# State and gate products of a gated state-space convolution block, issued as four 32x32 tiles each instead of one 32x128 tile

## The chip, the cores and the metric

The kernel runs on one core of one Trainium2 chip. The metric is the device time of one execution, in microseconds (us). The core has a matrix engine (TensorE, PE in the profile, with its weight loads shown apart as PEld), VectorE (DVE), ScalarE (ACT), GpSimd (POOL) and SyncE (SP), which issues the DMAs.

## The reference

The input x is 4 images of 128 channels of 96 x 96. It is normalised in groups of four channels, and then goes through the same one-dimensional block in four reading orders (rows, rows reversed, columns, columns reversed). The four results are joined by a 1x1 convolution and added to x. The block is, shortened:

```python
t = grouped1x1(x, in_proj_w, in_proj_b, 4)             # 128 -> 512 channels, 4 groups
u, gate = t[:, :256], t[:, 256:]
u = depthwise_conv5(silu(u), dw_w)
s = ssm_in_w @ u                                       # 32 channels
a = 0.999 + 0.0009 * sigmoid(ssm_delta_w @ u + ssm_delta_b)
bb, cc = tanh(ssm_b_w @ u + ssm_b_b), tanh(ssm_c_w @ u + ssm_c_b)
h = linear_scan(a, bb * s)                             # h[t] = a[t] h[t-1] + bb[t] s[t]
u = u + ssm_out_w @ (cc * h + ssm_d * s)               # 32 -> 256 channels: the state product
u = grouped1x1(u * sigmoid(gate), mix_w, mix_b, 4)     # gate: the gate product
return out_proj_w @ u
```

Mixing, output projection and joining are linear and stand behind each other, so the kernel multiplies their weights once (`w_fin`) and has one product per direction for them.

## The kernel before, in words

**Tiles.** A direction and its reverse are worked on together as sides s = 0 and 1. The sequence is cut into 384-element pieces, with four interleaved phases; one piece of both sides is a pair, and there are 192 pairs. All data are f32. Psum is one tile of eight banks, which the code rents out to named tenants (`TENANTS`, `BANKS`) and takes back when the last user has been written down.

**Products on PE.** A product writes 128 output channels of one bank. Most are issued through the helper `mm` (line 245), which writes 32 of them, so that four instructions make one product:

- the input projection F (`in_proj`), 32 input rows by 32 output columns a tile, 385 elements,
- the convolution C and its rest L (`conv`, `conv_less`), 128x32 and 64x32,
- the projections P to the small state (`proj`), 128x32,
- the last product W (`result`, weights `w_fin`), 128x32.

The state product S (`state`, line 866) and the gate product G (`gate`, line 872) are the exceptions: one instruction each, 32 input rows by all 128 output columns. A pair has four state products (S00, S01, S10, S11), on the four row groups of the array, each to its own bank. Half of the pairs also have four gate products (G00 to G11), again on the four row groups; for the other half the gates were stored and come back by DMA. ACT copies u to psum ahead of the state products (`under`, line 862), so that these add to it.

**Behind them.** ACT's `tanh_gate` (line 878) reads a gate product. DVE's `gating` (line 919) reads a pair of state products and multiplies by the gate; its result is what W reads one slot later. ACT's `take_result` (line 932) copies W's result, and POOL adds it to the output (line 972).

**Order.** Nothing is scheduled by a tool. The program is a list of slots, one for each pair, and in each slot a written order of operations (`PLAN`, four kinds of slot) is issued with a lag for each operation (`LAGS`); the start and the end have lists of their own (`START`, `END`). Each engine takes its instructions in the order in which they were issued, and semaphores hold what isn't ready. In the kind "gate" the part of the order that concerns PE reads `S11 S10 G00 S00 G01 G11 S01 G10`, then `W11 W10`: eight products of 32x128 in one stretch, on row groups 3, 1, 2, 0 and again 3, 1, 2, 0. In the kinds "front" and "none" the four state products of a pair stand together, without gate products.

## Time and profile before

| | |
|---|---|
| time, median of 3 runs | 1776.74 us (1774.55 to 1778.56) |
| span of the profiled execution, first to last instruction | 1770.6 us |
| mean granted TensorE clock | 0.994 |
| PE busy | 1747.7 us (99%) |
| DVE, ACT, POOL busy | 1516.8, 1486.1, 1394.0 us |
| matmul records on PE | 22584 |
| of these state products (L866) | 1536 records, 257.4 us busy |
| of these gate products (L872) | 768 records, 187.9 us busy |

The profiled execution's own time isn't told apart from the other runs; what lies around its span is the difference to them, 6.1 us at the median. In a row such as `128*32 128x384` the first pair is the tile's size on the array (rows by columns), the second the output. Busy time of a group is the union of its instructions, so where several run side by side it is far less than their count times the mean. A matmul of f32 is two records, its two passes, and each has a weight load of its own.

### The profile page before, as it was taken

The numbers are of one execution on the slowest core, as the hardware profiler recorded it, in microseconds if no ns is written. First come the engines' busy times: TensorE is split into PE (matmuls) and PEld (weight loads), VectorE is DVE, ScalarE is ACT, GpSimd is POOL, SyncE is SP. The second block draws the span as 40 slices with busy tenths as digits, with TensorE's granted clock in tenths as the row PEclk, the third lists the DMA queues.
The fourth block names the chain that finished last, engine by engine and source line by source line (L and its number), as shares of the span: only waits on it lengthen the run. The fifth ranks groups of instructions, "written<-read, shape, count | busy, mean of one in ns | idle before, by whom it ended". The sixth has DMA issues, their size and how long they took to land.

```text
span 1770.6 us, 54587 instructions
## 1 busy us (share of the span) xinstructions
PE 1747.7 (99%) x22584; PEld 638.7 (36%) x22584; DVE 1516.8 (86%) x1541; ACT 1486.1 (84%) x2571; POOL 1394.0 (79%) x1500
## 2 busy tenths in 40 slices
PE   6999999999999999999999999999999999999999
PEld 3333333333333333333333333333333333333333
DVE  4899988888788988988888988898888878888898
ACT  5788888888888888888888888888888888888875
POOL 4488888878778888788877888878777788887776
PEclk7999999999999999999999999999999999999999
DMA  7776676665987678564798657755589755656654
GB/s 229 180 238 232 180 227 187 201 204 175 295 261 235 209 209 241 182 204 165 218 293 264 231 188 227 223 179 198 165 257 278 250 193 181 209 159 198 215 190 165
DMA packets 183767, 377.69 MB, mean 213 GB/s; under 512 B 16736, under 2 KB 147040, under 8 KB 183520
## 3 DMA queue, kind: packets, MB, share of 16 engines
q1 hardware_dynamic: 183376, 374.16, 67.4%
q8 instruction: 178, 2.92, 0.7%
q14 instruction: 69, 0.57, 0.1%
q10 hardware_dynamic: 144, 0.04, 0.0%
HBM read 222.96 MB, written 151.18 MB: 211 GB/s over the span
## 4 chain that ended last, share of the span: by engine, by line
PE 91%; DMA 3%; ACT 2%; issue 1%; SPq 1%; DVE 1%; POOL 0%; ACTq 0%; POOLq 0%; DVEq 0%
PE psum L245 78%; PE psum L866 10%; PE psum L872 4%; DMA acc<-in_xr 2%; DMA out<-acc 1%; ACT gate L878 1%; POOL acc L972 0%; SPq L713 0%; DMA x_in<-in_xs 0%; ACT psum L862 0%; DVE u L919 0%; ACT sil L647 0%; DMA edge<-edge 0%; ACT u L748 0%; ACT t L812 0%
## 5 line engine op out<-in xcount | busy, mean ns | idle before, releaser
L785 DVE SCALAR_TENSOR_TENSOR psum<-sil,small,psum 128x768 f32<-128x768 f32 x576 | 588.1, 1022 | 56.1 <-ACT psum L783 38.1
L245 PE MATMUL psum<-u,w_fin 128*32 128x384 f32 x6144 | 580.0, 490 | 0.9
L245 PE MATMUL psum<-u,main 128*32 128x384 f32 x6144 | 562.2, 488 | 1.8 <-ACT gate L878 0.7
L972 POOL TENSOR_TENSOR acc<-ys,acc 128x384 f32<-128x384 f32 x365 | 422.1, 1165 | 155.2 <-ACT ys L932 76.8
L919 DVE SCALAR_TENSOR_TENSOR u<-gate,psum 128x768 f32<-128x768 f32 x376 | 346.0, 951 | 97.1 <-PE psum L866 69.9
L245 PEld LDWEIGHTS psum<-u,main 128*32 128x32 f32 x6144 | 186.6, 109 | 325.9 <-issue 216.0
L245 PEld LDWEIGHTS psum<-u,w_fin 128*32 128x32 f32 x6144 | 175.3, 109 | 342.8 <-issue 241.9
L862 ACT COPY psum<-u 128x768 f32<-128x768 f32 x352 | 278.1, 800 | 23.6 <-DVE u L766 8.4
L849 POOL TENSOR_TENSOR t<-t,t 64x384 f32<-64x384 f32 x192 | 235.1, 1225 | 68.4 <-DVE t L843 32.2
L245 PE MATMUL psum<-sil,band 128*32 128x384 f32 x3072 | 287.6, 490 | 1.1 <-ACT ys L932 1.1
L866 PE MATMUL psum<-t,main 32*128 32x384 f32 x1536 | 257.4, 530 | 1.3 <-ACT psum L862 1.3
L853 POOL TENSOR_TENSOR t<-t,t 64x384 f32<-64x384 f32 x192 | 236.9, 1234 | 7.6
L878 ACT ACTIVATE gate<-psum,bnorm 128x384 f32<-128x384 f32 x384 | 211.7, 577 | 33.4 <-PE psum L872 15.6
L826 POOL TENSOR_TENSOR t<-t,tm 64x384 f32<-64x384 f32 x191 | 196.0, 1026 | 51.1 <-ACT t L809 39.0
L823 POOL TENSOR_SCALAR t<-tm 64x384 f32<-64x384 f32 x191 | 179.7, 941 | 51.3 <-ACT tm L801 36.2
L647 ACT ACTIVATE sil<-psum,bnorm 128x385 f32<-128x385 f32 x384 | 200.4, 581 | 22.4 <-PE psum L245 21.8
L785 DVE SCALAR_TENSOR_TENSOR u<-sil,small,psum 128x768 f32<-128x768 f32 x192 | 194.7, 1014 | 18.2
L783 ACT ACTIVATE psum<-sil,small 128x768 f32<-128x768 f32 x192 | 173.7, 905 | 36.2 <-DVE u L919 31.5
L872 PE MATMUL psum<-x_in,wn 32*128 32x384 f32 x768 | 187.9, 516 | 0.2
L801 ACT ACTIVATE tm<-psum,small 128x384 f32<-128x384 f32 x192 | 112.5, 586 | 59.5 <-PE psum L245 57.2
L245 PEld LDWEIGHTS psum<-sil,band 128*32 128x32 f32 x3072 | 97.2, 110 | 152.4 <-issue 102.1
L932 ACT COPY ys<-psum 128x384 f32<-128x384 f32 x278 | 133.1, 479 | 21.3 <-POOL acc L972 10.9
(84 smaller groups left out, 1442.3 us busy)
## 6 DMA issues: line engine op xcount, KB each, us to landing
sil<-sil SPq DMA_DIRECT2D x128, 770.0 KB, 7.1
kept<-gate SPq DMA_DIRECT2D x80, 768.0 KB, 4.4
gate<-kept SPq DMA_DIRECT2D x76, 768.0 KB, 5.7
edge<-edge SPq DMA_DIRECT2D x96, 384.0 KB, 5.9
x_in<-in_xs SPq DMA_DIRECT2D x192, 96.2 KB, 3.5
edge<-sil SPq DMA_DIRECT2D x96, 192.5 KB, 3.9
acc<-in_xr SPq DMA_DIRECT2D x47, 384.0 KB, 7.8
out<-acc SPq DMA_DIRECT2D x44, 384.0 KB, 3.8
```

The costliest lines, as they stand in the source:

```text
L245: nc.tensor.matmul(o[r, : rhs.shape[-1]], lhsT, rhs, start=start, stop=stop, skip_group_check=True)
L647: nc.scalar.activation(sils[step][:, j, s, g, :], bank(frm)[:, : N + 1], AF.Silu, bias=bn[:, 1:2] if j else bn[:, 4 + g : 5 + g],)
L785: nc.vector.scalar_tensor_tensor(u_of(n)[:, :, 1, :] if k == K - 1 else part, src, w_tap[:, k : k + 1], part, ALU.mult, ALU.add,)
L826: engine.tensor_mul(scan_of(n)[0:64, pair_of(n)["p"], :], tbs[n][0:64, :], tms[n][0:64, :])
L849: engine.tensor_mul(ta[0:64, p, :], tbs[n][64:P, :], ta[64:P, p, :])
L853: engine.tensor_add(z, scans[n // R][0:64, pair_of(n)["p"], :], z)
L862: nc.scalar.copy(two(to), us[n][:, s])
L866: nc.tensor.matmul(bank(to)[:, :N], w_so[r, bass.ts(j, P)], tbs[n][r, :], start=not seeded(n), stop=True, skip_group_check=True)
L872: nc.tensor.matmul(bank(to)[:, :N], stats[pair_of(n)["b"]][0][r, s, :], x_in[s][r, q, off : off + N], start=True, stop=True)
L878: nc.scalar.activation(gates[n % 2][:, s, j, :], bank(frm)[:, :N], AF.Tanh, bias=bn[:, 2 + j : 3 + j], scale=0.5,)
L919: nc.vector.scalar_tensor_tensor(v, g, 1.0, two(frm), ALU.add, ALU.mult)
L972: nc.gpsimd.tensor_add(to, y, part)
```

## The change

Each state product and each gate product is issued as four tiles of 32 rows by 32 columns through `mm`, one for each quarter of the output channels. The operands, the banks, the place in the order and the flags of accumulation stay the same.

```diff
     def state(n, s, j, to):
         r = slice(64 * j + 32 * s, 64 * j + 32 * s + 32)
-        nc.tensor.matmul(bank(to)[:, :N], w_so[r, bass.ts(j, P)], tbs[n][r, :],
-                         start=not seeded(n), stop=True, skip_group_check=True)
+        for c in range(4):
+            mm(bank(to), c, w_so[r, j * P + 32 * c : j * P + 32 * c + 32], tbs[n][r, :],
+               not seeded(n), True)
 
     def gate(n, s, j, to):
         q, off = gate_at(pair_of(n))
         r = slice(64 * (1 - s) + 32 * j, 64 * (1 - s) + 32 * j + 32)
-        nc.tensor.matmul(bank(to)[:, :N], stats[pair_of(n)["b"]][0][r, s, :],
-                         x_in[s][r, q, off : off + N], start=True, stop=True)
+        for c in range(4):
+            mm(bank(to), c, stats[pair_of(n)["b"]][0][r, s, 32 * c : 32 * c + 32],
+               x_in[s][r, q, off : off + N], True, True)
```

On PE in a slot of the kind "gate", before: the run of eight products (t is the state, x_in with wn a gate product), between two pieces of W's work.

```order
L245 MATMUL psum<-u_732,w_fin 32x384 x4
L866 MATMUL psum<-t_5_913,main 128x384 x2
L872 MATMUL psum<-x_in_70,wn_330 128x384
L866 MATMUL psum<-t_5_913,main 128x384
L872 MATMUL psum<-x_in_70,wn_330 128x384
L872 MATMUL psum<-x_in_71,wn_330 128x384
L866 MATMUL psum<-t_5_913,main 128x384
L872 MATMUL psum<-x_in_71,wn_330 128x384
L245 MATMUL psum<-u_732,w_fin 32x384 x8
```

The same place on PE after the change:

```order
L245 MATMUL psum<-u_732,w_fin 32x384 x4
L245 MATMUL psum<-t_5_934,main 32x384 x8
L245 MATMUL psum<-x_in_70,wn_330 32x384 x4
L245 MATMUL psum<-t_5_934,main 32x384 x4
L245 MATMUL psum<-x_in_70,wn_330 32x384 x4
L245 MATMUL psum<-x_in_71,wn_330 32x384 x4
L245 MATMUL psum<-t_5_934,main 32x384 x4
L245 MATMUL psum<-x_in_71,wn_330 32x384 x4
L245 MATMUL psum<-u_732,w_fin 32x384 x8
```

Nothing has moved: eight instructions have become 32 at the same place, and the semaphores that a product waits for are on its first tile. On the other engines the order is the same as before.

On PE in slots of the kind "front", before: four state products in one run, between the convolution and its rest, and the projection F with 16 tiles close by.

```order
L245 MATMUL psum<-u_2918,main 32x384 x8
L245 MATMUL psum<-x_in_70,wn_330 32x385 x4
L245 MATMUL psum<-x_in_71,wn_330 32x385 x8
L245 MATMUL psum<-x_in_70,wn_330 32x385 x4
L245 MATMUL psum<-u_2918,main 32x384 x8
L245 MATMUL psum<-u_2289,w_fin 32x384 x8
L245 MATMUL psum<-sil_2596,band 32x384 x8
L866 MATMUL psum<-t_22_2490,main 128x384 x4
L245 MATMUL psum<-sil_2596,less 32x384 x8
```

After the change the row of L866 there is 16 tiles of line 245, the same number as F's 4 + 8 + 4 above it. Over the whole program PE's matmul instructions go from 11292 to 14748.

## The prediction

> **What bounds the kernel now.** I read the page's busy times first, then the chain that ended last, then the costliest groups.

> ```profile
> PE 1747.7 (99%) x22584; PEld 638.7 (36%) x22584; DVE 1516.8 (86%) x1541; ACT 1486.1 (84%) x2571; POOL 1394.0 (79%) x1500
> ...
> PE 91%; DMA 3%; ACT 2%; issue 1%; SPq 1%; DVE 1%; POOL 0%; ACTq 0%; POOLq 0%; DVEq 0%
> PE psum L245 78%; PE psum L866 10%; PE psum L872 4%; DMA acc<-in_xr 2%; DMA out<-acc 1%; ACT gate L878 1%; POOL acc L972 0%; SPq L713 0%; DMA x_in<-in_xs 0%; ACT psum L862 0%; DVE u L919 0%; ACT sil L647 0%; DMA edge<-edge 0%; ACT u L748 0%; ACT t L812 0%
> ...
> L866 PE MATMUL psum<-t,main 32*128 32x384 f32 x1536 | 257.4, 530 | 1.3 <-ACT psum L862 1.3
> L872 PE MATMUL psum<-x_in,wn 32*128 32x384 f32 x768 | 187.9, 516 | 0.2
> ```

> PE is busy 99% of the span and 91% of the chain. The changed products, L866 (state) and L872 (gate), are 10% and 4% of that chain. So what they gain or lose on PE goes almost straight into the time. The program has 768 state and 384 gate products, and the trace has 1536 and 768 records: each f32 product runs as two passes, each with its own weight load. After the change the 2304 pairs of load and matmul become 9216.

> How PE moves through such a run is the whole question. A run here is a stretch of instructions with one tile shape. Two runs can be compared directly: four state products of 32x128 (8 records), and 16 tiles of 32x32 in the projection F (32 records), which already has the form that state and gate products will get.

> ```profile
> 706.24 0.93 PE L866 MATMUL psum<-t,main 32*128 32x384 f32 x8
> 707.10 0.88 PE L245 MATMUL psum<-sil,less 64*32 64x384 f32 x16
> ...
> 701.36 0.95 PE L245 MATMUL psum<-x_in,wn 32*32 32x385 f32 x32
> 702.23 0.53 PE L245 MATMUL psum<-u,main 128*32 128x384 f32 x4
> ```

> The first column is the start, the second the length. From start to the start of the next shape the state run takes 707.10 - 706.24 = 0.86 us, the F run 702.23 - 701.36 = 0.87. So four products on four row groups cost the same array time in either form.

> **The change, term by term.**

> *Weight loads.* They get shorter and more numerous:

> ```profile
> L866 PEld LDWEIGHTS psum<-t,main 32*128 32x128 f32 x1536 | 99.2, 183 | 130.0 <-issue 69.4 <-ACT psum L862 12.0 <-POOL t L826 11.9
> L245 PEld LDWEIGHTS psum<-x_in,wn 32*32 32x32 f32 x3072 | 29.1, 104 | 66.9 <-issue 33.2 <-DVE u L919 13.8 <-ACT sil L647 5.6
> ```

> One load goes from 183 to 104 ns. Only the first load of a product that comes to an idle array is exposed, so a product that arrives late and alone gains 0.08 us. It pays for its four tiles starting one after the other: at 0.007 us a start that is 0.02 us, net -0.06 us.

> *Runs of four products (119 of them, by the program's order).* 93 of these run without a stall, and I take the difference of the two rows above, 0.875 - 0.858 before rounding: 93 x 0.017 = +1.6 us. In the other 25 that I could follow a product waited for another engine; where the last one did (as the gate product in the run at 291.03), the -0.06 applies, elsewhere about -0.02: together -0.7 us.

> *Runs of eight products (73).* This is the term that decides. One without a stall, and what ends it:

> ```profile
> 601.53 0.59 PE L866 MATMUL psum<-t,main 32*128 32x384 f32 x2
> 603.17 0.53 PE L245 MATMUL psum<-u,w_fin 128*32 128x384 f32 x4
> ...
> 602.53 1.17 ACT L878 ACTIVATE gate<-psum,bnorm 128x384 f32<-128x384 f32 x2 [0.39 <-PE psum L866]
> ...
> 603.17 0.16 PEld L245 LDWEIGHTS psum<-u,w_fin 128*32 128x32 f32 x8 [0.68 <-ACT gate L878]
> ```

> The run takes 603.17 - 601.53 = 1.64 us, and its end is the tanh of its first gate product, not PE. After the change the run has 32 tiles. The trace of before has one F run with more than 16 tiles and PE at its full clock, 20 tiles (40 records), early in the program:

> ```profile
> 52.42 0.21 PEld L245 LDWEIGHTS psum<-x_in,wn 32*32 32x32 f32 x24 [0.62 <-issue]
> ...
> 52.77 0.56 PE L245 MATMUL psum<-x_in,wn 32*32 32x385 f32 x12
> ...
> 52.98 0.13 PEld L245 LDWEIGHTS psum<-x_in,wn 32*32 32x32 f32 x5 [0.35 <-DVE u L766]
> ...
> 53.28 0.10 PEld L245 LDWEIGHTS psum<-x_in,wn 32*32 32x32 f32 x1
> ...
> 53.63 0.51 PE L245 MATMUL psum<-x_in,wn 32*32 32x385 f32 x3
> ...
> 53.66 0.48 PE L245 MATMUL psum<-x_in,wn 32*32 32x385 f32 x1
> 54.07 0.53 PE L245 MATMUL psum<-u,main 128*32 128x384 f32 x4
> ```

> ```profile
> 701.36 0.59 PE L245 MATMUL psum<-x_in,wn 32*32 32x385 f32 x14
> ...
> 701.36 0.62 PE L245 MATMUL psum<-x_in,wn 32*32 32x385 f32 x16
> ```

> 14 first passes end within 0.59 us, all 16 within 0.62: the last two took 0.016 each. With 32x128 a run of eight products is 32 instructions and never meets the limit.

> For 32 tiles without a stall: tile 18 enters 53.28 - 52.42 = 0.86 us after the run's start, tile 32 another 14 x 0.0165 (unrounded) = 0.23 later, and from the entry of the last tile (53.28 + 2 x 0.016 = 53.31) to the next shape it is 54.07 - 53.31 = 0.76. That makes 1.85 us against 1.64, so +0.21. Runs that already stalled lose less or the same; the larger part is held in the first half:

> ```profile
> 573.73 0.59 PE L866 MATMUL psum<-t,main 32*128 32x384 f32 x2
> 575.84 0.85 PE L245 MATMUL psum<-u,w_fin 128*32 128x384 f32 x8
> ...
> 574.35 0.29 PEld L866 LDWEIGHTS psum<-t,main 32*128 32x128 f32 x2 [0.31 <-ACT psum L862]
> ```

> Here the fourth product waits 0.62 us for ACT and the run takes 2.10. After the change tile 13 is held as long; its second pass ends 0.35 + 0.48 later, tile 30 enters 0.03 after that, at 1.48, tile 32 at 1.51, and the run ends at 2.27: +0.17. I went through the 73 runs with this rule, keeping each stall where it is from the run's start: 28 of the first kind (28 x 0.21 = 5.9), 27 of the second (27 x 0.17 = 4.6), and 18 in which a later product was already late (6 x 0.13 + 4 x 0.07 + 8 x 0.02 = 1.3). Sum +11.8 us. The first and last of the first two kinds:

> ```profile
> 105.36 0.59 PE L866 MATMUL psum<-t,main 32*128 32x384 f32 x2
> 107.01 0.53 PE L245 MATMUL psum<-u,w_fin 128*32 128x384 f32 x4
> ...
> 1680.96 0.59 PE L866 MATMUL psum<-t,main 32*128 32x384 f32 x2
> 1682.60 0.53 PE L245 MATMUL psum<-u,w_fin 128*32 128x384 f32 x4
> ...
> 1662.15 0.59 PE L866 MATMUL psum<-t,main 32*128 32x384 f32 x2
> 1664.26 0.53 PE L245 MATMUL psum<-u,w_fin 128*32 128x384 f32 x4
> ```

> (The second kind begins with the run at 113.90.)

> [...]

> *Runs of six products (15) and two single gate products.* By the same rule +0.6 and -0.1.

> *What moves on other engines.* The order there is unchanged; 13 tanh and 22 DVE instructions get one more semaphore to wait for, which I cost at nothing because what they name was a predecessor of their data before as well. SP's and POOL's queues are passed by nothing. In a run of eight the second half's results come later than PE's own delay (the state product that DVE's gating needs by up to 0.29 us in an unstalled run), and DVE does wait for such products:

> ```profile
> DVE u L919 <- PE psum L866: 70.5, 41, 3.3
> PEld psum L245 <- ACT gate L878: 69.5, 139, 1.0
> ```

> 41 such waits at up to 0.29 - 0.21 = 0.08 us bound this at +3 us; the lower bound is what ACT and DVE gain when PE is the slower one, below. I leave it at zero.

> *Sum.* 1.6 - 0.7 + 11.8 + 0.6 - 0.1 = +13.2 us on a span of 1770.6. The runs shown have a median of 1776.74, so 6.1 us lie around this span if the profiled execution was a median one; I carry the sum over: 1776.7 + 13.2 = 1790 us.

> **The rivals.**

> *A: no limit of 17 tiles for these products.* If tile 18's wait at 53.28 had another cause, a run of eight ends where the tanh ends it, and the late single products keep their -0.06. The same 73 runs then give -2.9 us, the others +0.2: 1774 us. For it: one long F run at full clock is thin evidence. Against: the 0.03 us after tile 1's end, the absence of a wait, and the 0.016 in two places. It decides from the point where the second half of a run enters before 0.86 us. Chance 0.12.

> *B: the loss is swallowed by stalls.* The eight-product runs hold about 17 us of stalls already (136 us in all, against 73 x 1.64 = 120). If PE's delay gave ACT that much of a lead, all would end at 1.85: 73 x 1.85 = 135, so -1.3, with the other terms (+1.4) 1777 us. Against: ACT is brought back into step in every slot by a wait for PE (0.39 us in the row of 602.53 alone). Chance 0.06.

> *C: the late second half drives the loop.* Where gating, the next slot's taps and ACT hang on the last state product, each of the 73 runs costs 0.29 instead of 0.16 us on average: 21 + 1.4, 1799 us. For it: the 70.5 us that DVE waits for state products. Against: only 41 waits, so a part at most. Chance 0.12.

> **How the numbers follow.** My forecast of 1790 has a chance of 0.70, between A's and C's ends by partial B or C: 1783 to 1797. Differences under 0.2% (3.6 us) are about what a measurement of this kernel can't tell from no change, as its runs lie 4 us apart. The range that leaves out no more than 2 in 10 is 1778 to 1801. Slower by over 0.2%: forecast and C, 0.82. Within 0.2%: most of A (its -2.7 is under 3.6) and B, 0.12. Faster: the rest of A, 0.06.

> **What would show it.** In the trace after, an unstalled run of eight should have its first 17 tiles loaded at once, tile 18 0.86 us after the start, the rest 0.016 apart, and last 1.85 us; a run of four 0.87. The idle time of w_fin's loads before L878 (69.5 us) should shrink, since PE itself now ends those runs. If runs of eight keep 1.64 us, A is right; if they take 1.85 and the time moves little, B; if PE waits more in slots after them, C. A slower rate of instructions than F shows, or transfers in the way of more instruction fetching, would make all of this wrong upwards.

## The result, and the profile after

The changed kernel takes 1790.76 us (median of 4, 1789.07 to 1793.05) against 1777.65 of the kernel before beside it: a ratio of 1.0071, 95% interval 1.0054 to 1.0087. It is slower, by 13.1 us where +13.2 was forecast. Another measurement further down gave 1.0069.

The page of the changed kernel, busy times and the chain by engine, with the state and gate products' groups from the view of groups by shape:

```profile
PE 1765.3 (99%) x29496; PEld 634.6 (35%) x29496; DVE 1517.8 (85%) x1541; ACT 1485.8 (83%) x2571; POOL 1395.3 (78%) x1500
...
PE 93%; DMA 3%; ACT 1%; SPq 1%; DVE 1%; POOL 0%; issue 0%; POOLq 0%; DVEq 0%; ACTq 0%
...
L245 PE MATMUL psum<-t,main 32*32 32x384 f32 x6144 | 270.6, 493 | 1.5 <-ACT psum L862 1.5
L245 PE MATMUL psum<-x_in,wn 32*32 32x384 f32 x3072 | 193.0, 491 | 0.0
```

PE's busy time went from 1747.7 to 1765.3 us, while DVE, ACT and POOL stay within 1.3 us of what they were. The work is the same, and PE holds it longer: the two groups were 257.4 and 187.9 us.

An eight-product run without a long stall, in the timeline of the changed kernel (start, length, then the group of instructions):

```profile
136.97 0.55 PE L245 MATMUL psum<-t,main 32*32 32x384 f32 x8
137.09 0.53 PE L245 MATMUL psum<-x_in,wn 32*32 32x384 f32 x4
...
138.41 0.53 PE L245 MATMUL psum<-x_in,wn 32*32 32x384 f32 x4
138.87 0.53 PE L245 MATMUL psum<-u,w_fin 128*32 128x384 f32 x4
...
137.82 0.10 PEld L245 LDWEIGHTS psum<-x_in,wn 32*32 32x32 f32 x1
```

The last row is the only weight load alive at that moment, that of the 18th tile: 137.82 - 136.97 = 0.85 us after the run's start, where the prediction put it at 0.86. The run takes 138.87 - 136.97 = 1.90 us, against the 1.64 of the kernel before and the 1.85 that were forecast.

A run of four products, and the L run behind it:

```profile
704.07 0.94 PE L245 MATMUL psum<-t,main 32*32 32x384 f32 x32
704.94 0.92 PE L245 MATMUL psum<-sil,less 64*32 64x384 f32 x16
705.79 1.50 PE L245 MATMUL psum<-u,w_fin 128*32 128x384 f32 x16
```

The run of four takes 0.87 us, as the F run promised. But the L run, which nobody touched, takes 705.79 - 704.94 = 0.85. In the kernel before it took 707.90 - 707.10 = 0.80:

```profile
707.10 0.88 PE L245 MATMUL psum<-sil,less 64*32 64x384 f32 x16
707.90 0.53 PE L245 MATMUL psum<-u,w_fin 128*32 128x384 f32 x4
```

### The profile page after: what moved, and what is told of

The parts are those of the page before. It is cut to its first block, busy times and chain, and to the rows that moved or that the text cites. A ratio compares the mean times of both kernels' runs of the same rounds, so it can differ in the third digit from the quotient of the medians.

```text
span 1789.8 us, 68446 instructions
## 1 busy us (share of the span) xinstructions
PE 1765.3 (99%) x29496; PEld 634.6 (35%) x29496; DVE 1517.8 (85%) x1541; ACT 1485.8 (83%) x2571; POOL 1395.3 (78%) x1500
## 4 chain that ended last, share of the span: by engine, by line
PE 93%; DMA 3%; ACT 1%; SPq 1%; DVE 1%; POOL 0%; issue 0%; POOLq 0%; DVEq 0%; ACTq 0%
PE psum L245 93%; DMA acc<-in_xr 2%; DMA out<-acc 1%; SPq L713 0%; DMA x_in<-in_xs 0%; POOL acc L974 0%; ACT sil L647 0%; ACT psum L862 0%; DMA edge<-edge 0%; SPq L940 0%; ACT t L812 0%; DVE u L766 0%; DVE u L921 0%; ACT t L809 0%; ACT t L830 0%
## 5 line engine op out<-in xcount | busy, mean ns | idle before, releaser
L245 PE MATMUL psum<-u,w_fin 128*32 128x384 f32 x6144 | 582.1, 490 | 1.0 <-DVE u L766 0.9
L245 PE MATMUL psum<-u,main 128*32 128x384 f32 x6144 | 563.9, 489 | 1.7 <-ACT gate L880 1.4
L245 PEld LDWEIGHTS psum<-u,main 128*32 128x32 f32 x6144 | 189.1, 110 | 326.1 <-issue 217.4
L245 PEld LDWEIGHTS psum<-u,w_fin 128*32 128x32 f32 x6144 | 176.4, 109 | 353.9 <-issue 237.8
L245 PE MATMUL psum<-x_in,wn 32*32 32x385 f32 (+1 forms) x6144 | 296.6, 498 | 2.4 <-DMA x_in<-in_xs 2.0
L862 ACT COPY psum<-u 128x768 f32<-128x768 f32 x352 | 278.2, 801 | 23.9 <-DVE u L766 7.5
L245 PE MATMUL psum<-sil,band 128*32 128x384 f32 x3072 | 288.9, 490 | 1.1 <-ACT ys L934 1.1
L245 PE MATMUL psum<-t,main 32*32 32x384 f32 x6144 | 270.6, 493 | 1.5 <-ACT psum L862 1.5
L826 POOL TENSOR_TENSOR t<-t,tm 64x384 f32<-64x384 f32 x191 | 195.2, 1022 | 60.9 <-ACT t L809 49.0
L647 ACT ACTIVATE sil<-psum,bnorm 128x385 f32<-128x385 f32 x384 | 200.2, 581 | 24.6 <-PE psum L245 21.9
L801 ACT ACTIVATE tm<-psum,small 128x384 f32<-128x384 f32 x192 | 112.3, 585 | 66.9 <-PE psum L245 63.7
L245 PEld LDWEIGHTS psum<-sil,band 128*32 128x32 f32 x3072 | 97.9, 110 | 153.3 <-issue 99.6
```

Source lines behind the costliest of these rows:

```text
L245: nc.tensor.matmul(o[r, : rhs.shape[-1]], lhsT, rhs, start=start, stop=stop, skip_group_check=True)
L647: nc.scalar.activation(sils[step][:, j, s, g, :], bank(frm)[:, : N + 1], AF.Silu, bias=bn[:, 1:2] if j else bn[:, 4 + g : 5 + g],)
L826: engine.tensor_mul(scan_of(n)[0:64, pair_of(n)["p"], :], tbs[n][0:64, :], tms[n][0:64, :])
L862: nc.scalar.copy(two(to), us[n][:, s])
```

## Two theories, and what told them apart

Theory Q is the prediction's reading of the run of 20 tiles, whose 18th loads 0.86 us after the start: PE holds 17 f32 tiles, 68 load and matmul instructions, and takes the next when the oldest is done, so that a longer run is held up. Theory T is the plain alternative: every further instruction has a price wherever it stands, 13.1 us spread over 1152 products. The sizes of the runs separate the two.

**Half as many tiles.** Two tiles of 32x64 for a product, so that a run of eight is 16 tiles.

```diff
-        for c in range(4):
-            mm(bank(to), c, w_so[r, j * P + 32 * c : j * P + 32 * c + 32], tbs[n][r, :],
-               not seeded(n), True)
+        for c in range(2):
+            h = slice(64 * c, 64 * c + 64)
+            nc.tensor.matmul(bank(to)[h, :N], w_so[r, j * P + 64 * c : j * P + 64 * c + 64],
+                             tbs[n][r, :], start=not seeded(n), stop=True, skip_group_check=True)
```

(The gate products likewise.)

> Every state and gate product as two tiles of 32x64 instead of four of 32x32, nothing else changed. Theory Q (PE holds about 17 f32 matmuls with their loads, 68 instructions, and takes the next when the oldest is done): a run of eight products is 16 tiles and fits, so the loss of the four-tile form goes away as a whole, 1774 to 1779 us, and an unstalled run of eight keeps 1.64 us. Theory T (each further tile has a price wherever it stands; the four-tile form adds 3 instructions to each of 1152 products for 13.1 us, 0.0038 us each): one more instruction for each product costs a third, +4.4 us, 1782 us.

Measured: 1775.88 us (12 runs) against 1777.19, ratio 0.9993, interval 0.9984 to 1.0002. The loss is gone as a whole, not by two thirds. A run of eight in the kernel with two tiles for a product:

```profile
375.25 0.55 PE L868 MATMUL psum<-t,main 32*64 32x384 f32 x4
...
376.88 0.53 PE L245 MATMUL psum<-u,w_fin 128*32 128x384 f32 x4
```

376.88 - 375.25 = 1.63 us, where the kernel before took 1.64. Theory T falls here: twice the instructions cost nothing in a run of 16 tiles. So does another rival, that a tile is held up when it comes back to a part of the array that an earlier tile of the run has used. In the changed kernel the 17th tile is the first to do so, here it is the 9th (both belong to the fifth product), and nothing is lost. In the run of 20 tiles, by its order in `START` (F3, F0, F1, F3, F0), tiles 17 to 20 come back to the parts of tiles 5 to 8, which the prediction called free; tile 17 loads there at 53.01, while the second pass of tile 5, begun at 52.79, takes 0.48.

**One part alone: only runs of four.** Four tiles where no gate product shares the run, one tile elsewhere. The diff is against the changed kernel; the gate products are one tile again, which it leaves out.

```diff
+    def with_gates(n):
+        return gated(n) or (n + 1 < NPAIR and gated(n + 1))
     def state(n, s, j, to):
         r = slice(64 * j + 32 * s, 64 * j + 32 * s + 32)
+        if with_gates(n):
+            nc.tensor.matmul(bank(to)[:, :N], w_so[r, bass.ts(j, P)], tbs[n][r, :],
+                             start=not seeded(n), stop=True, skip_group_check=True)
+            return
         for c in range(4):
...
```

> Four tiles of 32x32 only for state products that stand in runs without gate products (some 90 runs of four), everything else one tile of 32x128. Theory Q: 16 tiles fit, so only the +0.017 us of an unstalled run of four remains, less what late products gain: +1 us, 1778 to 1779. Theory T: some 360 of the 1152 products, +4.1 us, 1782.

Measured: 1779.02 us against 1777.19, ratio 1.0010, interval 0.9999 to 1.0021. That is +1.8, nearer to Q's +1 than to T's +4.1. A part of the difference to +1 is in the L runs, as the view of groups by shape shows for this kernel and for the other part below:

```profile
L245 PE MATMUL psum<-sil,less 64*32 64x384 f32 x1536 | 86.1, 498 | 0.0
```

```profile
L245 PE MATMUL psum<-sil,less 64*32 64x384 f32 x1536 | 84.7, 498 | 0.0
```

L is busy for 86.1 us with tiles in the runs of four (and in the changed kernel), and for 84.7 with tiles only in the runs with gates, as before the change. Sixteen tiles are 64 instructions, of the 68 in the 17 tiles that load ahead of the gap in longer runs, so that I read the 1.4 us as most of L's instructions entering only as the state tiles are done. The kernel with two tiles for a product agrees: there a run of four is 8 tiles, and the view has the same row for it as the second one above, 84.7 us. In the changed kernel 33 of the 36 L runs that stand right behind state products take 0.84 or 0.85 us, the other three 0.81 or 0.82. No run was made for this reading alone.

**The other part: only runs with gate products.** The condition of the diff above turned round (`if not with_gates(n)`), and gate products in four tiles.

> The other part: four tiles of 32x32 for all gate products and for the state products that stand in one run with them, state products of the other runs in one tile of 32x128. Theory Q: nearly the whole loss, +12 us, 1789 to 1790, with the 18th tile of an unstalled run loading 0.86 us after the run's start. Theory T: some 790 products, +9 us, 1787, and no gap behind the 17th tile.

Measured: 1785.39 us against 1777.19, ratio 1.0046, interval 1.0033 to 1.0059: +8.2 us. The gap behind the 17th tile is there:

```profile
164.77 0.55 PE L245 MATMUL psum<-t,main 32*32 32x384 f32 x8
...
166.67 0.53 PE L245 MATMUL psum<-u,w_fin 128*32 128x384 f32 x4
...
165.63 0.10 PEld L245 LDWEIGHTS psum<-x_in,wn 32*32 32x32 f32 x1
```

165.63 - 164.77 = 0.86, and the run takes 1.90. The total was below both expectations, though, and nearer to T's +9 than to Q's +12: here it is the gap that speaks for Q, not the time. And the two parts made 0.56% where the whole had made 0.71%. So both were run once more, side by side.

> The changed kernel itself once more, side by side with its larger part, because the two parts measured one by one (+0.10% and +0.46%) come to 0.56% where the whole was 0.71%. Theory Q, by the sum of its terms: +13.2 us, ratio 1.0074. If the parts are all there is: 1.0056. The intervals so far hold both.

> Four tiles only in the runs with gate products, once more beside the whole. Theory Q: the whole less 1 to 2 us, ratio 1.0065. If part of the loss in these runs is taken back by the engines that wait elsewhere, it stays near the 1.0046 of the first time.

Measured: the whole 1789.17 us against 1777.67, ratio 1.0069 (1.0057 to 1.0082); the part with gates 1786.03, ratio 1.0049 (1.0036 to 1.0062). So runs with gates carry 8.2 and 8.4 us in the two measurements, runs of four some 1.8, and 2 us between their sum and the whole lie within the intervals. The part with gates is again nearer to its first 1.0046 than to the 1.0065 that Q gave. It is smaller than the +12 of the prediction's term, although its runs of eight are as long as in the whole. What gives the rest back outside of these runs was not isolated.

**No run longer than four products.** If length is the cause, breaking the runs in two should free the tiles from their loss. In the written order of the slots with gates, four matmuls of W and the copy of their result were moved between the fourth and the fifth product, once with one tile and once with four tiles for a product.

```diff
-        ... C1 DEC CT C0 SC W00 L T3 SS T4 UND0 W01 BS S11
-        E AFTER SCAN1 S10 G00 CH UC YS0 S00 G01 G11 TH0 ...
+        ... C1 DEC CT C0 SC W00 L T3 SS T4 UND0 BS S11
+        E AFTER SCAN1 S10 G00 CH UC S00 W01 YS0 G01 G11 TH0 ...
```

> The kernel before with one row of the written order changed in slots with gate products: four matmuls of W (the second half of W's side 0) now stand between the fourth and the fifth of the eight products, so that no run has more than four products. Each slot gets one or two more changes of shape at 0.1 to 0.15 us: 72 slots, +7 to +20 us against the kernel before, 1785 to 1798. Both theories agree; the run is there to be compared with the next.

> The kernel with four tiles of 32x32 for every state and gate product, with the same row of the written order changed, so that no run has more than 16 tiles. Theory Q: the limit is never met, so it stands within -1 to +5 us of the same order with 32x128 tiles (the +0.017 us of some 260 runs of four). Theory T: the number of tiles is what it was, so it is 13 us above the same order with 32x128 tiles.

Measured against 1777.17 us: one tile 1856.1, ratio 1.0448 (1.0434 to 1.0463); four tiles 1860.82, ratio 1.0471 (1.0456 to 1.0485). Between them lie 4.7 us by the medians: at the upper end of Q's -1 to +5. The intervals of the two ratios leave about 0 to 8 us, which keeps out T's 13. In this order PE stands still before gate products, though, for 25.9 us in all with one tile and 26.0 with four, against 0.2 in the kernel before, which could hide a part of any loss, so that this pair weighs less than the kernel with two tiles for a product. My expectation of the new order itself was badly off, +79 us instead of 7 to 20. Its 0.1 to 0.15 us for a change of shape was my estimate, and no run shows it; what the runs show is these waits. In the one-tile kernel PE waits in the middle:

```profile
376.07 0.85 PE L245 MATMUL psum<-u,w_fin 128*32 128x384 f32 x8
377.63 0.66 PE L872 MATMUL psum<-x_in,wn 32*128 32x384 f32 x2 [0.70 <-ACT ys L930]
...
377.62 0.29 PEld L872 LDWEIGHTS psum<-x_in,wn 32*128 32x128 f32 x3 [1.40 <-ACT ys L930]
...
PEld psum L872 <- ACT ys L930: 37.8, 43, 1.4
```

The fifth product waits for ACT to copy the result of the very W that now stands just ahead of it, which I read as the hand-over of a psum bank that both use in turn; no run was made for this alone. The last row is from the waits; before it read:

```profile
PEld psum L872 <- ACT ys L930: 9.4, 26, 0.7
```

**Only the gate products.** One part of the diff alone, so that shapes alternate inside a run.

```diff
     def gate(n, s, j, to):
...
-        nc.tensor.matmul(bank(to)[:, :N], stats[pair_of(n)["b"]][0][r, s, :],
-                         x_in[s][r, q, off : off + N], start=True, stop=True)
+        for c in range(4):
+            mm(bank(to), c, stats[pair_of(n)["b"]][0][r, s, 32 * c : 32 * c + 32],
+               x_in[s][r, q, off : off + N], True, True)
```

> Only the gate products as four tiles of 32x32, state products in one tile of 32x128, so that the two shapes alternate within a run of eight (S S G S G G S G). Both theories expect a large loss from a third cause, the wait for an empty array at each change of shape, which the trace of before shows as 0.41 us from the last matmul's start to the first load of the next shape: pieces S S, G, S, G G, S, G of about 0.84, 0.78, 0.84, 0.81, 0.84, 0.78 us make 4.9 us instead of 1.64 to 2.1, about +3 us for each of 73 runs and some +1 us for each of the 45 other runs with gates: +230 us, near 2010 us.

Measured: 2190.94 us, ratio 1.2331 (1.2291 to 1.237). The run itself is as forecast:

```profile
654.16 0.91 PE L866 MATMUL psum<-t,main 32*128 32x384 f32 x4
655.01 0.85 PE L245 MATMUL psum<-x_in,wn 32*32 32x384 f32 x8
655.78 0.91 PE L866 MATMUL psum<-t,main 32*128 32x384 f32 x2
656.62 0.88 PE L245 MATMUL psum<-x_in,wn 32*32 32x384 f32 x16
657.43 0.91 PE L866 MATMUL psum<-t,main 32*128 32x384 f32 x2
658.26 0.85 PE L245 MATMUL psum<-x_in,wn 32*32 32x384 f32 x8
659.04 0.53 PE L245 MATMUL psum<-u,w_fin 128*32 128x384 f32 x4
```

Six pieces of 0.77 to 0.85 us make 4.88. The forecast of the total, 2010, was 180 us too low: other engines wait more for the products, and the granted clock was lower.

```profile
DVE u L920 <- PE psum L866: 247.1, 128, 5.7
ACT gate L879 <- PE psum L245: 202.1, 211, 3.5
...
core 0: 2181.7 us, clock 0.926
```

DVE's wait for state products grew from 70.5 to 247.1 us, and the mean granted clock fell from 0.994 to 0.926. How the 180 us divide among the waits and the clock, and what lowered the clock, was not measured.

## Why the prediction was right, point by point

*The limit of 17 tiles* was right, and the runs show it in two ways: the 18th tile comes 0.85 to 0.86 us after the run's start, and the loss disappears when the run has 16 tiles (1775.88 us against 1777.19), although the instructions per product are still doubled. Rival A, no such limit, would have needed runs of eight at 1.64 us and the time near 1774; it falls. What the limit counts, instructions or matmuls, is not settled: 16 f32 matmuls are 64 instructions in every kernel here.

*The sum of the runs of eight* came out as forecast, but by terms that offset each other. Added up from the timelines of all 73 runs, from each run's start to the next shape, they took 136.3 us before and 148.2 after: +11.9 against +11.8. The 28 unstalled runs, however, went to 1.90 and not to 1.85 us. Before rounding that is +0.265 for each, 7.4 us together where the sum had 5.9. The other 45 runs lost 4.4 us, where the sum had 4.6 + 1.3 = 5.9 (the last term adds up to 1.2 as it is written, a difference that matters to nothing here).

The 0.05 that an unstalled run takes longer than forecast comes behind the 18th tile, whose load at 137.82 was on time. The loads of the seventh and the eighth product and of the next shape in the same run:

```profile
137.97 0.18 PEld L245 LDWEIGHTS psum<-t,main 32*32 32x32 f32 x8
138.06 0.18 PEld L245 LDWEIGHTS psum<-x_in,wn 32*32 32x32 f32 x8
138.87 0.16 PEld L245 LDWEIGHTS psum<-u,w_fin 128*32 128x32 f32 x8 [0.63 <-ACT gate L880]
```

Tile 25 comes 137.97 - 137.82 = 0.15 after the 18th, where seven steps of 0.0165 make 0.12. Tile 29 comes 0.09 later still, where four steps make 0.07. The first tiles of these two products are thus 0.05 late together, and behind the last tile the forecast's 0.76 holds. What holds them is not shown. It is not the third product, although this one is late too: it waits for two semaphores, and its first tile starts 0.12 us into the run (137.09 against 136.97) instead of 0.01 before the change (601.54 against 601.53). In five other runs that take 1.90 the third product starts after 0.05 us, as here:

```profile
1483.03 0.55 PE L245 MATMUL psum<-t,main 32*32 32x384 f32 x8
1483.08 0.53 PE L245 MATMUL psum<-x_in,wn 32*32 32x384 f32 x4
...
1484.93 0.53 PE L245 MATMUL psum<-u,w_fin 128*32 128x384 f32 x4
```

On the other side stalls have shrunk: 136.3 - 73 x 1.64 = 16.6 us of them before, 148.2 - 73 x 1.90 = 9.5 after, and 48 of the 73 runs now take 1.90. The forecast had 73 x 0.21 - 11.8 = 3.5 of these 7 us, by its smaller terms for stalled runs. The rest is rival B in part, and it offsets the 73 x 0.05 = 3.7 by which the unstalled run was set too short. That a stall keeps its place in the run was a wrong assumption for some of them. The prediction's own example, the run at 573.73 with 2.10 us, is this one after the change, the 25th of the 73 in both:

```profile
580.51 0.55 PE L245 MATMUL psum<-t,main 32*32 32x384 f32 x8
...
580.81 0.58 PE L245 MATMUL psum<-t,main 32*32 32x384 f32 x12
...
582.46 0.53 PE L245 MATMUL psum<-u,w_fin 128*32 128x384 f32 x4
```

Its fourth product comes 0.30 us after the start, where it had come after 0.62 (of which its row shows 0.31 as the wait for ACT), and the run takes 1.95 where 2.27 was forecast. So the mechanism was right, and the 0.1 us by which the totals agree is luck.

*Rival C*, the loop driven by late second halves, doesn't show: DVE's wait for state and gate products together reads 80.0 us in the trace after, against 70.5 + 2.6 = 73.1 before, and the total is 8 us below C's 1799. The waits for gate products before, and the wait after:

```profile
DVE u L919 <- PE psum L872: 2.6, 6, 0.7
...
DVE u L921 <- PE psum L245: 80.0, 71, 3.4
PEld psum L245 <- ACT gate L880: 71.3, 152, 2.1
```

The last row corrects another sign that the prediction named: the load idle time before the tanh releases should have shrunk from 69.5 us, and it didn't. This idle time of the load side runs on while matmuls are still busy (the loads of 138.87 show 0.63 of it, while the last matmuls of the run, 0.53 long, started at 138.41), and so it said little about who ends a run.

*Runs of four*: +0.9 was forecast; by the same adding up the 119 took 105.56 us before and 106.84 after, +1.3. *Runs of six and the two single gate products*: +0.5 forecast, runs of six found at +0.1. *The L runs* were left out of the sum: +1.4 us, a cost outside the changed code, and by my reading of the same cause. Together the terms found in the traces are 11.9 + 1.3 + 0.1 + 1.4 = 14.7 us, against the timed 13.1, whose interval is 9.6 to 15.5.

*The profiled execution.* The prediction took 6.1 us to lie around the span. The changed kernel's profiled execution took 1791.52 us at a span of 1789.8, so only 1.7 lie around it; the profiled execution of before, if the same lies around it, was thus a quick one, near 1772, below every timed run of that kernel on record (the lowest took 1774.18). Read from trace to trace the loss is therefore 19 us, and only the timed medians give the 13. The forecast carried its sum over to the median, so this changed nothing in it.

## What to carry to other kernels

Count what stands in a row, not only what the array can do at once. A product cut into more tiles cost next to nothing here where the whole run had 16 f32 tiles: such runs lost 0.01 us each (1.3 us in 119 runs), and those behind which L stood held it up by another 0.04. An unstalled run of 32 tiles, whose 18th came only after 0.85 us, lost 0.26 (1.90 against 1.64). Two 64-column tiles for a product did the same work without loss (ratio 0.9993). Look for the longest run of the form you want in the trace you have: one run of 20 tiles at the start of the program held the answer. And cut all products of a run in the same way or none: alternating shapes made the kernel take 23% longer here (2190.94 us against 1777.19).

## What the runs showed that was not expected

A run made the next one slower without touching it: the L run of eight matmuls took 0.85 instead of 0.80 us behind 16 tiles. A wait in the second half of a long run cost nothing: in the run from 344.52 to 346.43 the fifth product's first tile comes only at 345.52, 1.00 us after the start, and the run takes 1.90 us before rounding, like an unstalled one. And moving four matmuls of W behind four products in the order cost 79 us; a wait for ACT's copy, which the diff doesn't show, grew with it, from 9.4 to 37.8 us.
